# Tokens' scale inside the Gelu, small sums of the second mixer on GpSimd, a new order of the mixer's period and tail, explicit last features, and a later check of the first recurrence

## The chip, the cores and the metric

The kernel runs on one core of a Trainium2 chip. The metric is the time of one execution on the device in microseconds (us). Three runs of the kernel before took 1125.45, 1125.59 and 1127.28 us; the median is 1125.59. One more run was taken with the hardware profiler; it took 1123.8 us with a profiled span of 1122.0 us, and all stretches and durations below are of that run.

The engines are named as in the profile: PE does matrix products (PEld is its loading of weights), DVE is the vector engine, ACT the scalar engine, which applies functions such as Gelu or Sigmoid, POOL is GpSimd, and SP issues the transfers. PE writes to PSUM, and DVE and ACT take its results from there.

## The reference

The input x has 4 batches of 32 tokens, each an image of 128 x 128, all in fp32. Two layers follow each other:

```python
x = x + codano(_ln_c(x), ...)          # layer 0: attention on Fourier modes, then a mixer
t = t + ffn(_ln_t(t), W, V, ...)       # layer 0: x W, batch norm, a recurrence with a sigmoid
x = x + conv(_ln_c(x), ...)            # layer 1: upsample, leaky relu, downsample
t = t + ffn(_ln_t(t), W, V, ...)       # layer 1: the same with other weights
```

The part that the change touches most is the mixer inside `codano`:

```python
m = instance_norm(attn, norm2_g, norm2_b)
m = fno_layer(m, mixer_w1, mixer_skip_w1, mixer_skip_b1, (H, W), norm=(mixer_norm_g1, mixer_norm_b1), act=_gelu)
m = fno_layer(m, mixer_w2, mixer_skip_w2, mixer_skip_b2, (H, W), norm=(mixer_norm_g2, mixer_norm_b2))
out = instance_norm(m, mixer_out_g, mixer_out_b) + attn
```

An `fno_layer` is a convolution on 32 x 17 Fourier modes, normalised per image, plus a pointwise skip. In `ffn`, the features `x W` of all tokens are normalised by a mean and variance over everything, so the recurrence `y = sigmoid(wx + y V^T)` can't start before the last feature's statistics are in.

## The kernel before

The activations stay on the chip in `XA`, [128 rows, 4 batches, 32 tokens, 128 columns]. The features of the recurrences and its states lie in `WX`, a view of `WXY`. Stages follow each other: attention (to about 236 us), a short stretch that works out the scalars of the mixer (`f1`, `r1`, `e1`, `k1` and others), the mixer with the first features beside it (250 to 557 us), the first recurrence (to 621 us), the convolutions with the second features beside them (to about 1039 us), and the second recurrence with the output.

**The mixer** goes over 8 chunks of 4 tokens (`TM`), each of 16 images. For chunk c, `first_mixer` adds, per image, the tokens times a scale per image (`f1B`, a column for each image) to the inverse transform in PSUM (L1133, DVE, one operation per image), and applies Gelu (L1134, ACT, one operation for the four images of a batch). `transform` takes Z to its modes `Fz` (L1160, L332 on PE, copies on ACT at L1162 and L1166). `squares` (ACT, L1141) and `half_squares` (DVE, L1147) sum the squares of Z, each for half of the images. `second_mixer` is a generator of seven steps: from `Fz` and the squares it works out some numbers per image (`v2`, `x2`, `mz`, `d`, `al`, `ga`, `de`), with two inverse roots on POOL (L226, `pow`) and complex products on POOL (L1203 to L1205, L1220 to L1222), and then `G[c]`, the modes of the chunk's result (L1232, L1236 and L1237). `first_halves(of_G(c), 0)` takes G back on PE (L345), `inverse_rows` gives images in PSUM (L360), `tokens_added` adds the attention (L1246), and `residual` writes the result into XA (L1253 and L1255, two DVE operations per image). The residuals of chunk c are done during chunk c + 1 (its number is `S`).

**The first features** run behind: `chunk_stats` and `chunk_norm` give mean and inverse root of each row of a finished chunk, `rows` normalises (L290 on ACT, and L288 on DVE for some of the last tokens), `turn` transposes on PE (L296), `turned` copies (L304), `multiply` is the product (L310), and `multiplied` takes its statistics (L313, DVE) and copies it to `WX` (L317, ACT). Token u = 4(c - 2) is handled in chunk c, so two more rounds, c = 8 and c = 9, finish chunk 7's residuals and the last features.

**What sets the order.** Inside `with in_order()` PE, DVE, ACT and POOL each execute the instructions in the order in which the Python loop emits them; the loop's text is the plan. Elsewhere a scheduler orders instructions by priority. Tiles with the same tag share a fixed number of buffers: `ps4` has four PSUM buffers `big`, `psf` has one each of `t` and `w`, and `ps4s` one each of `inv10` and `inv11`.

**The recurrence** (`Recurrence.scan`) splits the 128 steps into four pieces that start from a guess and warm up over 12 steps (`WARM`); a check at its end compares where the pieces meet (L1692 to L1697 on DVE) and sets a flag that a fallback would read. The object `f1` for the second recurrence is built ahead of the first one's scan and transposes its weights then (L274, L275, copy at L277).

**The convolutions** go in units of half a token; with `at` other work is put beside a unit. The second features use the same functions `turn`, `turned` and `multiply` with one PSUM buffer `w` in the pool `ps_w` for all products.

Of the kernel before, what the change touches and what calls it, by code (L numbers as in the profile page):

```python
# [142 lines left out]
def _network(  # L143
# [249 lines left out]
    f1B, r1B = (mw.tile([P, P], F32, name=k) for k in ("f1B", "r1B"))  # L393
    q1L = mw.tile([P, NT], F32, name="q1L")
    sg, nsg = (mw.tile([P, 1], F32, name=k) for k in ("sg", "nsg"))
# [595 lines left out]
    with (  # L991
# [17 lines left out]
        def besides(n):  # L1009
# [3 lines left out]
        var, v0, r1, s, a, f1, e1, k1, q1, sv, s0 = (  # L1013
            one(k) for k in ("var", "v0", "r1", "s", "a", "f1", "e1", "k1", "q1", "sv", "s0"))
# [50 lines left out]
        tt(f1, a, scalar("mixer_skip_w1"), ALU.mult)  # L1065
# [4 lines left out]
        tt(e1, e1, a, ALU.mult)  # L1070
# [4 lines left out]
        stt(HT[:, :, :, :KW], Ym, f1, GT, ALU.mult, ALU.add)  # L1075
        nc.vector.tensor_copy(HT[:, 0, 16, 0:1], k1)
# [3 lines left out]
        for v, dst in ((f1, f1B), (r1, r1B)):  # L1080
            d = np_.tile([P, P], F32, tag="dg", name="dg")
            ts(d, ident, v, None, ALU.mult)
            p = ps3.tile([P, P], F32, tag="dg", name="ps_dg")
            mm(p, ones_sq, d, start=True, stop=True)
            nc.scalar.copy(dst, p)
# [10 lines left out]
    with (  # L1096
# [10 lines left out]
        bsum, w2d, w2s = (m1.tile([P, 1], F32, name=k) for k in ("bsum", "w2d", "w2s"))  # L1107
# [3 lines left out]
        tt(w2s, w2, w2, ALU.mult)  # L1111
        chunks = NT // TM
# [11 lines left out]
        def first_mixer(c, b, p2):  # L1124
# [5 lines left out]
            z = Z[c][:, b]  # L1130
            for i in range(TM):
                j = b * NT + c * TM + i
                stt(z[:, i], XA[:, b, c * TM + i, :], f1B[:, j : j + 1], p2[:, i], ALU.mult, ALU.add)  # L1133
            nc.scalar.activation(z, z, AF.Gelu)  # L1134


        def squares(c, images):
            for k in images:
                b, i = divmod(k, TM)
                junk = m2.tile([P, P], F32, tag="junk", name="junk")  # L1140
# [28 lines left out]
        def second_mixer(c):  # L1169
# [16 lines left out]
            for b in range(NB):  # L1186
# [7 lines left out]
            s2, s3, vm, d, al, ga, de = (  # L1194
                m1.tile([P, TM], F32, tag=k, name=k) for k in ("s2", "s3", "vm", "d", "al", "ga", "de"))
            rsqrt(s2, v2, 1e-5, TM)

            pool = nc.gpsimd.tensor_tensor
# [8 lines left out]
            ts(d, mz, nsg, None, ALU.add)  # L1207
            tt(d, d, d, ALU.mult)
            tt(vm, e2[:, :, 0], e2[:, :, 1], ALU.add)
            stt(d, vm, 1.0 / P**2, d, ALU.mult, ALU.subtract)  # L1210
            ts(d, d, w2s, None, ALU.mult)
            ts(x2, x2, w2d, None, ALU.mult)
# [9 lines left out]
            pool(G[c][:, :, 2], g1, g2, ALU.add)  # L1222
            yield True
            ts(s3, s3, scalar("mixer_out_g"), None, ALU.mult)
            ts(ga, s3, w2, None, ALU.mult)
# [3 lines left out]
            tt(al, s3, s2, ALU.mult)  # L1229
            tt(al, al, q1L[:, tr], ALU.mult)  # L1230
            ts(G[c][:, :, 0], G[c][:, :, 2], -1.0, None, ALU.mult)
            tt(G[c], G[c], al.unsqueeze(2).unsqueeze(3).broadcast_to([P, TM, 3, KH]), ALU.mult)  # L1232
            tt(de, ga, mz, ALU.mult)
            ts(de, de, -1.0, bsum, ALU.mult, ALU.add)
            tt(de, de, q1L[:, tr], ALU.mult)
            stt(G[c], Y3[:, :, :, tr].rearrange("p r k t -> p t r k"), scalar("attn_norm_g"), G[c], ALU.mult, ALU.add)  # L1236
            stt(G[c][:, :, 1, 16], de, dcm, G[c][:, :, 1, 16], ALU.mult, ALU.add)  # L1237
            ps = psf.tile([P, 512], F32, tag="t", name="ps_gb")[:, : NB * TM]
            mm(ps, ones_sq, ex.rearrange("p b t -> p (b t)"), start=True, stop=True)
            yield True  # L1240
            gB[c] = m2.tile([P, NB * TM], F32, tag="gB", name="gB")
# [6 lines left out]
        def residual(c, b, p2):  # L1248

            for i in range(TM):  # L1250
# [28 lines left out]

        def first_halves(g, t0):  # L1280
            return inverse_columns(lambda q, i, k: g(q, t0 + i, slice(k, k + 2)), ps4s, m2)
# [15 lines left out]
        def rows(t):  # L1297
            if t in range(NT) and inputs is not None:
                xn[t] = inputs.normalised(t, *norm.pop(t), vector=(t >= NT - 8 and t % 4 > 0 or t >= NT - 4))
# [22 lines left out]
        with in_order():  # L1322
# [3 lines left out]
            for c in range(chunks + 2):  # L1326
                I, S, u = c < chunks, c - 1 if 0 < c <= chunks else None, 4 * (c - 2)
                if c == chunks:
                    inputs is None or inputs.use(m2, ps4, ps4, ("big", "big"))
                multiply(u - 2)  # L1330
                turn(u - 1)
                if I:
                    first_mixer(c, 0, early_.pop((c, 0)))
                    squares(c, range(0, 2))
                    first_mixer(c, 1, early_.pop((c, 1)))
                if c in affines:
                    next(affines[c])
                if I:
                    first_mixer(c, 2, early_.pop((c, 2)))
                turned(u - 1)  # L1340
                multiplied(u - 2)
                if I:
                    first_mixer(c, 3, early_.pop((c, 3)))
                if S is not None:
                    p2 = inverse_rows(QG[S], 0, ps4)
                if I:
                    first = transform(c)
                    next(first)
                if S is not None:
                    tokens_added(S, 0, p2[0])  # L1350
                multiply(u - 1)
                if I:
                    next(first)
                    squares(c, range(2, 6))
                    half_squares(c)
                    next(first)
                    next(first)
                    next(first)
                    second = second_mixer(c)
                    next(second)  # L1360
                if S is not None:
                    residual(S, 0, p2[0])
                if I:
                    squares(c, range(6, 8))
# [632 lines left out]
```

## Time and profile before

| Stretch (us) | What | PE | DVE | ACT | POOL | Granted TensorE clock |
|---|---|---|---|---|---|---|
| 252.70 to 277.00 | chunk 0 | 18.62 | 16.16 | 9.36 | 4.68 | 0.67 |
| 305.00 to 342.00 | chunk 2 | 30.91 | 27.74 | 17.11 | 7.95 | 0.72 |
| 411.50 to 445.60 | a steady chunk | 28.41 | 29.33 | 20.23 | 7.58 | 0.85 |
| 506.20 to 532.20 | last residuals | 16.10 | 20.32 | 9.98 | 2.91 | 0.96 |
| 620.00 to 640.00 | the convolutions start | 13.78 | 17.48 | 6.77 | 3.33 | 0.91 |

The numbers under the engines are busy microseconds in the stretch. G of chunks 0 to 7 is ready at about 272.7, 299.7, 335.6, 369.2, 403.7, 437.9, 472.1 and 506.2 us, so a steady chunk takes about 34.15 us. A chain of waits is read by asking for each operation what it waited for last. A row of the groups by form names line, engine, operation, what it writes and reads, the shape, the count, and after the bar the total busy time in us and the mean in ns, then idle time ahead of it. A row of the timeline has start and length in us.

### The profile page before, as it was taken

The numbers are of one execution on the slowest core, as the hardware profiler recorded it, in microseconds if no ns is written. First come the engines' busy times: TensorE is split into PE (matmuls) and PEld (weight loads), VectorE is DVE, ScalarE is ACT, GpSimd is POOL, SyncE is SP. The second block draws the span as 40 slices with busy tenths as digits, with TensorE's granted clock in tenths as the row PEclk, the third lists the DMA queues.
The fourth block names the chain that finished last, engine by engine and source line by source line (L and its number), as shares of the span: only waits on it lengthen the run. The fifth ranks groups of instructions, "written<-read, shape, count | busy, mean of one in ns | idle before, by whom it ended". The sixth has DMA issues, their size and how long they took to land.

```text
span 1122.0 us, 18048 instructions
## 1 busy us (share of the span) xinstructions
PE 960.9 (86%) x6398; PEld 691.9 (62%) x6398; DVE 812.7 (72%) x2744; ACT 630.9 (56%) x1496; POOL 124.4 (11%) x130
## 2 busy tenths in 40 slices
PE   3999799757687777876599799999999999998896
PEld 3565566645454544542288577777777777775785
DVE  6985777756878898887488855666656666554897
ACT  3756466634347555563488444655556564655764
POOL 1000000101212122121100112020111102010000
PEclk9999799967869888889799999999999999999898
DMA  9640000010101011100000000001000000004444
GB/s 238 143 79 25 1 1 1 1 38 1 38 20 39 20 39 38 51 26 20 0 1 1 1 19 29 20 20 30 19 20 20 27 21 20 20 28 156 168 161 140
DMA packets 68964, 48.82 MB, mean 44 GB/s; under 512 B 4417, under 2 KB 63809, under 8 KB 68801
## 3 DMA queue, kind: packets, MB, share of 16 engines
q1 hardware_dynamic: 68529, 47.31, 14.8%
q8 instruction: 53, 0.87, 0.3%
q0 software_dynamic: 288, 0.01, 0.2%
q10 hardware_dynamic: 48, 0.26, 0.1%
q14 instruction: 46, 0.38, 0.1%
HBM read 30.68 MB, written 16.88 MB: 42 GB/s over the span
## 4 chain that ended last, share of the span: by engine, by line
PE 53%; DVE 22%; ACT 7%; issue 4%; POOL 4%; POOLq 0%; ACTq 0%; DVEq 0%
PE ps_scan L1657 9%; PE ps_up L1788 7%; PE ps_dn L1800 6%; PE ps_wx L310 4%; PE ps_dn L1809 3%; PE ps_up L1777 3%; PE pm L918 3%; PE ps_st L1160 3%; DVE XA L1255 3%; PE ps_y L976 2%; POOL c_r L226 2%; PE ps_inv L345 2%; DVE XA L1253 2%; DVE f_st L251 2%; DVE bn L313 2%
## 5 line engine op out<-in xcount | busy, mean ns | idle before, releaser
L1791 DVE SCALAR_TENSOR_TENSOR U<-ps_up,above 128x512 f32<-128x512 f32 x128 | 86.6, 690 | 89.9 <-ACT above L1790 89.9
L1788 PE MATMUL ps_up<-q,WXY 128*128 128x512 f32 x256 | 122.2, 599 | 6.9 <-ACT q L1780 6.5
L1800 PEld LDWEIGHTS ps_dn<-WXY,U 128*128 128x128 f32 x1024 | 124.4, 192 | 3.3
L1800 PE MATMUL ps_dn<-WXY,U 128*128 128x128 f32 x1024 | 124.6, 275 | 0.0
L1658 DVE SCALAR_TENSOR_TENSOR ps_scan<-WXY,bs,ps_scan 128x128 f32<-128x128 f32 x352 | 104.4, 353 | 10.4 <-PE ps_scan L1657 8.2
L310 PE MATMUL ps_wx<-xt,wvt 128*128 128x512 f32 x128 | 75.8, 677 | 32.1 <-ACT xt L304 27.8
L290 ACT ACTIVATE xn<-XA,f_o,f_r 128x128 f32<-128x128 f32 x178 | 75.6, 489 | 21.8 <-DVE f_o L259 21.8
L226 POOL TENSOR_TENSOR f_r<-rs_e,neg_half 128x16 f32<-128x16 f32 (+2 forms) x18 | 47.3, 2626 | 365.3 <-DVE rs_e L225 365.3
L1790 ACT ACTIVATE above<-ps_up 128x512 f32<-128x512 f32 x128 | 74.3, 597 | 23.6 <-PE ps_up L1788 23.6
L317 ACT COPY WXY<-ps_wx 128x512 f32<-128x512 f32 x64 | 37.3, 583 | 74.0 <-DVE bn L313 73.7
L1802 ACT COPY q<-ps_dn 128x512 f32<-128x512 f32 x64 | 37.5, 586 | 71.8 <-PE ps_dn L1800 71.8
L1777 PEld LDWEIGHTS ps_up<-WXY,XN 128*128 128x128 f32 x256 | 49.1, 192 | 33.6 <-issue 15.1
L1788 PEld LDWEIGHTS ps_up<-q,WXY 128*128 128x128 f32 x256 | 43.6, 190 | 40.1 <-issue 24.5
L1777 PE MATMUL ps_up<-WXY,XN 128*128 128x256 f32 x256 | 66.6, 383 | 0.0
L1809 PE MATMUL ps_dn<-q,WXY 128*128 128x256 f32 x256 | 66.0, 380 | 0.0
L313 DVE BATCH_NORM_STATS2 bn<-ps_wx 128x6 f32<-128x512 f32 x64 | 44.4, 694 | 26.7 <-PE ps_wx L310 26.6
L251 DVE BATCH_NORM_STATS2 f_st<-XA 128x6 f32<-128x128 f32 x256 | 57.8, 281 | 1.6
L1809 PEld LDWEIGHTS ps_dn<-q,WXY 128*128 128x128 f32 x256 | 46.1, 190 | 16.4 <-issue 12.0
L713 PE MATMUL ps_st<-cst,XA 128*128 128x130 f32 x256 | 43.3, 308 | 14.2 <-ACT XA L696 11.0
L304 ACT COPY xt<-ps_xt 128x512 f32<-128x512 f32 x64 | 37.6, 589 | 29.5 <-PE ps_xt L296 27.1
L310 PEld LDWEIGHTS ps_wx<-xt,wvt 128*128 128x128 f32 x128 | 22.8, 200 | 48.0 <-ACT xt L304 35.8
L713 PEld LDWEIGHTS ps_st<-cst,XA 128*128 128x128 f32 x256 | 35.0, 204 | 27.3 <-ACT XA L696 12.2
(410 smaller groups left out, 2076.2 us busy)
## 6 DMA issues: line engine op xcount, KB each, us to landing
XA<-in_x_dram SPq DMA_DIRECT2D x16, 512.0 KB, 7.3
xin<-in_x_dram SPq DMA_DIRECT2D x32, 256.0 KB, 3.2
turned<-XA SPq DMA_DIRECT2D x32, 256.0 KB, 2.3
XA<-turned SPq DMA_DIRECT2D x8, 1024.0 KB, 15.0
out_dram<-res SPq DMA_DIRECT2D x64, 128.0 KB, 2.1
WXY<-dd SPq DMA_DIRECT2D x4, 544.0 KB, 10.9
WXY<-md SPq DMA_DIRECT2D x4, 144.0 KB, 6.0
WXY<-m1d SPq DMA_DIRECT2D x1, 544.0 KB, 11.0
```

The costliest lines, as they stand in the source:

```text
L251: nc.vector.bn_stats(st[:, j * NB + b, :], XA[:, b, t, :])
L290: nc.scalar.activation(xn[:, b, :], XA[:, b, t, :], AF.Identity, bias=n(b), scale=r(b))
L310: mm(self.held[t], self.t[:, 0, :], xt, start=True, stop=True)
L713: mm(p[:, i, :], XA[:, b, t0 + j + i, :], cst[:, C_E : C_E + 130], start=True, stop=True)
L1657: mm(p4, self.t[:, 1, :], prev, start=True, stop=True)
L1658: stt(p4, WX[:, :, h, :], s[:, 0:1], p4, ALU.mult, ALU.add)
L1777: mm(p[:, b, :], XN[u // 2][:, (u % 2) * H2 + b, :], UR.rearrange("p r q -> p (r q)"), start=True, stop=True)
L1788: mm(p, UC[:, s, :], q, start=True, stop=True)
L1790: nc.scalar.activation(above, p, AF.Relu, scale=1.0 - SLOPE)
L1791: stt(U[:, s], p, SLOPE, above, ALU.mult, ALU.add)
L1800: mm(p[:, r, b, :], U[:, s, b, r * P : (r + 1) * P], DC[:, s, :], start=(s == 0), stop=(s == 1))
L1809: mm(p, DR[:, r, :], q[:, r], start=(r == 0), stop=(r == 1))
```

## The change

1. The scale per image moves from the sum to the Gelu: `first_mixer` adds `mixer_skip_w1` times the tokens to PSUM in one DVE operation per batch, and sixteen ACT operations apply Gelu with a scale (`aB`) and a bias (`k1`) that are pointers. Accordingly `f1` and one product of `e1` go, and H's constant mode is 0 where it was `k1`.
2. In `second_mixer` the sums for `d`, `x2`, `al` and `de` go from DVE to POOL; only two of G's three planes are scaled and added, and the third is their negative afterwards.
3. The loop runs over the 8 chunks alone, with its calls in another order. What followed as rounds 8 and 9 is written out as a tail. There the last chunk's features go in halves by batch pairs (`last_norm`, `last_rows`), each product covers two tokens of two batches, products use further PSUM buffers, and a Sigmoid of one column is run on ACT ahead of the last transposes. All rows of the features before that are normalised on ACT.
4. The last four products of the second features use one PSUM buffer each (`up1`, `up20`, `up21`, `up1`).
5. `check` becomes a function of its own; for the first recurrence it is emitted beside unit 5 of the convolutions. `f1` is built after the first scan is emitted.

```diff
-            for i in range(TM):
-                j = b * NT + c * TM + i
-                stt(z[:, i], XA[:, b, c * TM + i, :], f1B[:, j : j + 1], p2[:, i], ALU.mult, ALU.add)
-            nc.scalar.activation(z, z, AF.Gelu)
+            stt(z, XA[:, b, c * TM : c * TM + TM, :], scalar("mixer_skip_w1"), p2, ALU.mult, ALU.add)
+            for i in range(TM):
+                j = b * NT + c * TM + i
+                nc.scalar.activation(z[:, i], z[:, i], AF.Gelu, bias=k1, scale=aB[:, j : j + 1])
...
-            ts(d, mz, nsg, None, ALU.add)
-            tt(d, d, d, ALU.mult)
-            tt(vm, e2[:, :, 0], e2[:, :, 1], ALU.add)
-            stt(d, vm, 1.0 / P**2, d, ALU.mult, ALU.subtract)
-            ts(d, d, w2s, None, ALU.mult)
-            ts(x2, x2, w2d, None, ALU.mult)
+            pools(d, mz, nsg, None, ALU.add)
+            pool(d, d, d, ALU.mult)
+            pools(d, d, w2s, None, ALU.mult)
+            pool(ex2, e2[:, :, 0], e2[:, :, 1], ALU.add)
+            pools(ex2, ex2, w2v, None, ALU.mult)
+            pool(d, ex2, d, ALU.subtract)
+            pools(x2, x2, w2d, None, ALU.mult)
             yield True
...
+            pool(al, s2, q1L[:, tr], ALU.mult)
+            pools(al, al, scalar("mixer_out_g"), None, ALU.mult)
+            yield True
+
+            ts(ga, s3, scalar("mixer_out_g"), w2, ALU.mult, ALU.mult)
...
-            ts(G[c][:, :, 0], G[c][:, :, 2], -1.0, None, ALU.mult)
-            tt(G[c], G[c], al.unsqueeze(2).unsqueeze(3).broadcast_to([P, TM, 3, KH]), ALU.mult)
-            tt(de, ga, mz, ALU.mult)
-            ts(de, de, -1.0, bsum, ALU.mult, ALU.add)
-            tt(de, de, q1L[:, tr], ALU.mult)
-            stt(G[c], Y3[:, :, :, tr].rearrange("p r k t -> p t r k"), scalar("attn_norm_g"), G[c], ALU.mult, ALU.add)
-            stt(G[c][:, :, 1, 16], de, dcm, G[c][:, :, 1, 16], ALU.mult, ALU.add)
+            tt(al, al, s3, ALU.mult)
+            pool(de, ga, mz, ALU.mult)
+            pools(de, de, -1.0, bsum, ALU.mult, ALU.add)
+            pool(de, de, q1L[:, tr], ALU.mult)
+            pools(de, de, dcm, None, ALU.mult)
...
+            Gc = G[c][:, :, 1:3]
+            tt(Gc, Gc, al.unsqueeze(2).unsqueeze(3).broadcast_to([P, TM, 2, KH]), ALU.mult)
+            stt(Gc, Y3[:, 1:3, :, tr].rearrange("p r k t -> p t r k"), scalar("attn_norm_g"), Gc, ALU.mult, ALU.add)
+            tt(G[c][:, :, 1, 16], G[c][:, :, 1, 16], de, ALU.add)
+            ts(G[c][:, :, 0], G[c][:, :, 2], -1.0, None, ALU.mult)
...
@@ the middle of the loop, new order @@
                 if S is not None:
                     p2 = inverse_rows(QG[S], 0, ps4)
+                    tokens_added(S, 0, p2[0])
+                next(first)
                 if S is not None:
+                    tokens_added(S, 1, p2[1])
                 multiply(u - 1)
                 if S is not None:
                     residual(S, 0, p2[0])
+                    residual(S, 1, p2[1])
+                    xin.pop((S, 0))
+                load(c, 0)
+                next(first)
+                squares(c, range(0, 3))
+                next(first)
+                half_squares(c)
+                next(first)
+                multiplied(u - 1)
+                squares(c, range(3, 5))
+                if S is not None and inputs is not None:
+                    chunk_stats(S, 0)
+                next(first)
+                next(second)
+                squares(c, range(5, 8))
...
+                next(second)
+                if S is not None:
+                    residual(S, 2, p2[0], range(2))
+                next(second)
...
+                rows(u)
+                next(second)
+                if S is not None:
+                    residual(S, 2, p2[0], range(2, 4))
+                rows(u + 1)
...
@@ the end of the tail @@
+                next(halves_[0])
+                first = last_rows(S, 0, 0), last_rows(S, 0, 2)
+                inputs.use(m2, ps4, ps4s, ("big", "inv11"))
+            multiplied(u + 2)
+            multiply(u + 3)
+            if inputs is not None:
+                nc.scalar.activation(m1.tile([P, 1], F32, name="one"), bsum, AF.Sigmoid, scale=0.0)
+                turns = [inputs.turn(xn_) for xn_ in first]
+                multiplied(u + 3)
...
@@ second features and check @@
+                if t >= NT - 4:
+                    f1.use(wk, ps_t, ps_c1, ("t", ("up1", "up20", "up21", "up1")[t - NT + 4]))
                 f1.products(t, xt.pop(t))
...
+            at(5, f0.check)
...
             f1.scan(output)
+            f1.check()
```

## The prediction

> **What bounds the kernel now.** I read the busy line of the page first: no engine is full over the whole span, so the stages must be looked at one by one.
>
> ```profile
> PE 960.9 (86%) x6398; PEld 691.9 (62%) x6398; DVE 812.7 (72%) x2744; ACT 630.9 (56%) x1496; POOL 124.4 (11%) x130
> ```
>
> Then the busy times of single stretches: one steady period of the mixer loop, then the stretch from the last residual to the first recurrence.
>
> ```profile
> 445.60:479.80 34.20, 28.42 (x252) 17.90 (x252) 29.44 (x119) 20.23 (x53) 7.73 (x11) 0.85 0.17 47
> ...
> 532.20:557.00 24.80, 14.60 (x38) 6.86 (x38) 11.16 (x36) 11.69 (x25) 3.11 (x2) 0.74 0.00 0
> ```
>
> After the length come the busy times of PE, PEld, DVE, ACT and POOL with their counts, then the granted clock. In the loop DVE works 29.4 of 34.2 us; in the tail nobody works half the time and TensorE is granted 0.74. The chain of waits within one period says what the period is made of (time, length, who):
>
> ```profile
> 438.06 3.69 PE ps_inv L345 x64
> ...
> 445.02 0.71 DVE bn L313
> ...
> 446.88 1.12 PE ps_wx L310 x2
> ...
> 448.44 1.06 PE ps_inv L360 x4
> 449.50 1.93 PE ps_st L1160 x16
> ...
> 455.61 1.09 PE ps_pf L332 x28
> 456.72 0.38 ACT Fz L1166
> 457.13 0.42 ACT sq L1174
> 457.58 0.30 DVE sq L1176
> ...
> 471.83 0.24 DVE G L1237
> 472.20 0.87 PE ps_inv L345 x9
> ```
>
> It is a ring of 34.1 us: G ready (438.0), its transform on PE, the next Z, Gelu, two forward transforms, Fz, small sums, G again (472.1). Until 457.5 it passes between PE, ACT and DVE; from there it is DVE in order. So it counts when Fz is ready and what DVE does on the path, not busy time alone. Last, the rows that price the change, from the groups by form, and the end of the second features in the timeline:
>
> ```profile
> L1133 DVE SCALAR_TENSOR_TENSOR Z<-XA,f1B,ps_inv 128x128 f32<-128x128 f32 x128 | 34.6, 341 | 9.6 <-PE ps_inv L360 9.6
> L1134 ACT ACTIVATE Z<-Z 128x512 f32<-128x512 f32 x32 | 19.8, 625 | 7.1 <-DVE Z L1133 6.4
> L290 ACT ACTIVATE xn<-XA,f_o,f_r 128x128 f32<-128x128 f32 x178 | 75.6, 489 | 21.8 <-DVE f_o L259 21.8
> ...
> 1033.21 1.90 PE L310 MATMUL ps_wx<-xt,wvt 128*128 128x512 f32 x2 [1.41 <-ACT WXY L317]
> 1035.15 0.70 DVE L313 BATCH_NORM_STATS2 bn<-ps_wx 128x6 f32<-128x512 f32 x1 [2.61 <-PE ps_wx L310]
> 1035.89 0.58 ACT L317 COPY WXY<-ps_wx 128x512 f32<-128x512 f32 x1 [2.73 <-DVE bn L313]
> 1036.52 0.50 PEld L310 LDWEIGHTS ps_wx<-xt,wvt 128*128 128x128 f32 x2 [2.98 <-ACT WXY L317]
> ```
>
> The last four lines are one turn of a ring through a single PSUM buffer: product, statistics, copy, next product, 3.3 us each.
>
> **What the Trainium skill says.** "ScalarE: Activation LUTs", section "What ACT_TABLE_LOAD costs": an ACTIVATE costs 186 ns plus 0.833 ns per element, 93 ns more per pointer operand, and neighbours overlap by 93. That is 479 ns for 128 columns with scale and bias as pointers; the trace agrees (L290, 489 ns; four in 1.64 us, 0.385 apart). The same section gives about 1283 ns for a table load; this trace has 1.28 us at 559.78. "GPSIMD Engine Reference", section 3.1, puts a two-input GpSimd operation at about 2.6 cycles per element of 1.2 GHz, 277 ns for 128 columns; the 128x128 products here (456 ns) then leave an estimated 0.18 us fixed. "TensorE: Matmul & The Clock Gate", Part 1, says that idle stretches halve the clock; here the same pair of products takes 1.12 us after short gaps and 2.08 at 534 us after 7.2 us of idling.
>
> **The change part by part.** All sums are against the profiled span, 1122.0 us; that run took 1123.8, the others 1125.45 to 1127.28 with median 1125.59. I put G at zero in the period that begins at 438.0.
>
> *Gelu with scale and bias.* DVE: 16 operations at 0.27 apart (4.3 us) become four of 128x512, as L1791 (690 ns, 0.62 apart): 2.5. DVE wins 1.8 us a chunk. ACT: four of 0.63 become sixteen 0.385 apart, 6.2 us. ACT has room in sum (20.2 of 34.2), but Gelu lies on the ring. Z starts at 7.6 as before; ACT is free at 8.7; three images, a copy of xt and one of a product, the last image: 8.7+4.65+1.0+1.6 = 15.9, before 13.1.
>
> *Order of the period.* In the new order of instructions both residuals of the first pair, the half squares and the statistics of a product come ahead of the ring's small sums on DVE. The first residual waits for PE (product 8.8, turn, inverse rows to 11.4, tokens added 12.3), where before DVE had the half squares to do. From 12.3 DVE runs 2.6+2.6+2.3+0.6 = 8.1 to 20.5. ACT's copy of that product is queued ahead of Fz, so Fz (pf is ready at 19.6) waits for it: copy 0.5, two squares 1.0, Fz and its square 0.8: 22.9, before 19.5. The parts take 1.35: 24.3, before 20.8.
>
> *Small sums on GpSimd.* DVE loses about 1.0 us (L1207 to L1212) and 1.1 us in the part with G (128x384 to 128x256, three de operations, one al). But the sums become a wait. DVE from 24.3: two residual images 1.3, sa and rs_e 0.3, GpSimd starts at 26.1; pow 1.0, three products 1.4 (as 462.47 to 464.86), then seven operations of 128x4, the last of which gives x2. DVE has two images (1.3) and two small operations, then stands at x2. The trace has no such operation: a memset of 128x4 takes 0.10 (lower end), the 128x128 product 0.456 (upper end). I take 0.20 from the 0.18 above: 1.4, x2 at 29.9, a wait of 2.2 us. Behind DVE's wait stand the last residual, G, and with G all of PE's next inverse. Then three sums and rs_e 0.7, residual 2.6 (beside it pow 1.0, products 1.45, two al operations 0.4 on GpSimd), ga and ex 0.4, al 0.2, G 0.45+0.6+0.2+0.25: 35.4.
>
> So the steady period is 35.4 against 34.15: **+1.25**. DVE's work falls from 30.8 (dense, gaps of issue included) to 26.9, its idle rises from 3.3 to 8.5. Six periods (chunks 2 to 7): +7.5. Chunk 1 has no features: ACT's longer Gelu +1.5, residuals leave the path, +0.6. Chunk 0 has nothing to hide with: Gelu +1.7, squares and sums on the path, +2.9. Two small operations ahead of the loop go: -0.4. **Loop: +10.6.** Loads of xin, on SP's queue, move with the residuals that free their buffers; they land in 3.2 us, half a period ahead of use, so nothing. The statistics of the chunk before rows are needed run beside PE's transform of G: nothing.
>
> *The tail.* Before: G of the last chunk 506.2, last residual ends 532.2, last statistics 556.7, thus 50.5. After: PE brings the first residual at 12.2; DVE is then dense, four residuals 10.4, three statistics 1.8, first half's row statistics 2.8: 27.3. Second half: 2.8, GpSimd pow of 8 columns 1.64 and 0.35 around it: 32.0. ACT is then the limit: four rows to 33.4, copy 0.5, table load and its dummy 1.55, copy 0.5, two turned copies 1.05 to 37.0, four rows to 38.6, four half copies to 40.0, two turned copies to 41.0, last product 42.6, statistics 43.4. **-7.1.** The spans of the first halves are hidden by DVE's residuals.
>
> *Start of the recurrence.* The table load (1.28) no longer stands between DVE at 559.7 and the first step, and a weight copy (L277, 0.43, 0.3 effective) leaves DVE: **-1.6**. The copy and its two transposes move into the first steps, where PE waits for ACT anyway.
>
> *Check of the first recurrence.* Of its operations the order keeps the first (differences, product) at the old place; comparison and reduction (0.42 and 0.67) leave the path between 622.6 and 625.9: **-1.0**. They land in the convolutions, where PE is busy 98% and DVE 63%: nothing.
>
> *Last four features.* With own PSUM banks the products don't wait for copies. Rows of the last image are normalised by 1027.1 as now; then xt copies 1027.7 and 1029.3 (two product copies between them), product 1030.4, statistics 1031.2, before 1039.37: **-8.1**. Output then starts at 1053.7 instead of 1061.7; the 8 MB read into XA is issued by 1039.6 and DMA is quiet from 1053, so it isn't in the way.
>
> Sum: 10.6-7.1-1.6-1.0-8.1 = **-7.2**, a span of 1114.8; from the median, **1118.4 us**.
>
> **Rivals.** (1) *Slower: the GpSimd sums decide.* Each 0.1 us more per small operation adds 0.7 at x2 and 0.2 at al, over 8 chunks 7.2 us. At 0.30 the change is even; at 0.40 it costs +7.2, 1132.8; at the upper end 0.456, 1136.8. For it: scalar pointers, and DVE and GpSimd hinder each other here (L1214 takes 0.41 beside a product, 0.21 alone). Against: the fixed part above. At the lower end 0.10 the time is 1111.2.
> (2) *The period does shrink.* If the waits I place at 12.3, 22.9 and 29.9 mostly vanish, DVE's 26.9 and the idle of before (3.3) bound it: about 31, six times -3.2, chunk 0 and 1 even: -19 and the ends -17.8: 1089. For it: that DVE is busiest. Against: the ring above.
> (3) *The ends are hidden anyway.* PE at half clock (2.1 us per product) or another buffer takes half of the 17.8: -8.9+10.6 = +1.7, 1127.3. For it: 0.74 granted there. That the change doesn't do what it says is excluded for instructions, since the built order shows each part, for time it is this case.
>
> **How the numbers follow.** What this kernel's measurement can tell from no change is 0.2%, 2.3 us. Forecast 0.54 (own range 1110 to 1125), rival 1 0.24, rival 2 0.12, rival 3 0.10. Faster: 0.47+0.12+0.02 = 0.61; same: 0.06+0.04+0.05 = 0.15; slower: 0.01+0.20+0.03 = 0.24. The range 1103 to 1135 leaves out rival 2 and the top of rival 1.
>
> **What would show it.** Right: sixteen Gelus near 0.49 us, DVE idle before x2 with GpSimd as releaser about 2 us per chunk, G to G near 35.4, the last four feature products about 1 us apart where they were 2.5 to 3.3, no table load at the first recurrence. Wrong: periods under 34, small GpSimd operations at 0.3 us or more, or features still 2.5 us apart at the end.

## The result, and the profile after

The changed kernel takes 1131.25 us (median of 8 runs, 1129.52 to 1132.40), the kernel before 1127.2, measured beside it: a ratio of 1.0034, 95% interval 1.0022 to 1.0046. It is slower by 0.3%; 1118.4 and "faster" were forecast. The two profiled executions differ by 5.7 us (1122.0 and 1127.7), where the forecast's sum was -7.2, and the loss is not where that sum would put it. Marks for the table are the first transform of H1 by 56 products, the first product on G of the last chunk, the last statistics (`mv`) of the first and of the second features, and the first `c_o` of the convolutions:

| stretch | before | after | difference | forecast |
|---|---|---|---|---|
| start to H1 | 246.60 | 250.21 | +3.6 | -0.4 |
| H1 to the last G (loop) | 259.75 | 275.78 | +16.0 | +11.0 |
| last G to first `mv` (tail) | 50.39 | 44.14 | -6.3 | -7.1 |
| `mv` to first `c_o` (recurrence, check) | 70.26 | 67.28 | -3.0 | -2.6 |
| `c_o` to second `mv` (convolutions, last features) | 412.37 | 406.66 | -5.7 | -8.1 |
| second `mv` to the end | 82.63 | 83.63 | +1.0 | 0 |
| sum | 1122.0 | 1127.7 | +5.7 | -7.2 |

The busy line of the page shows that what was meant to move did move:

```profile
PE 960.8 (85%) x6398; PEld 689.9 (61%) x6398; DVE 788.4 (70%) x2561; ACT 668.4 (59%) x1605; POOL 155.1 (14%) x235
```

DVE has 24.3 us less to do, ACT 37.5 and GpSimd 30.7 more. The stretch table of one steady period and of the tail after the last residual (17.40 us, where it was 24.80) says what came of it (from, to, length, then busy PE, PEld, DVE, ACT, POOL, the granted clock):

```profile
452.62:488.99 36.37, 28.63 (x252) 17.96 (x252) 26.51 (x96) 24.03 (x65) 11.46 (x23) 0.86 0.16 45
552.70:570.10 17.40, 10.19 (x31) 5.21 (x29) 9.78 (x33) 11.05 (x27) 1.99 (x2) 0.80 0.00 0
```

The period grew from 34.2 to 36.4 us while DVE's work in it fell from 29.4 to 26.5. So DVE waits. The chain of waits of this period has a stretch that was not there before:

```profile
478.47 1.01 POOL s L226
479.48 0.51 POOL g L1202
479.99 0.42 POOL g L1203
480.41 0.07 issue
480.48 0.46 POOL G L1204
480.93 0.30 POOL d L1206
...
482.75 0.28 POOL sa L1212
483.03 0.02 issue
483.06 0.17 DVE vm L1216
```

GpSimd does a pow, three products of 128x128 and then seven sums of 128x4 in its own order; the last of them (x2, a part of the tile `sa`) releases DVE. The groups by form say how long each takes and how long DVE stood:

```profile
L1133 ACT ACTIVATE Z<-Z,k,aB 128x128 f32<-128x128 f32 x128 | 50.7, 486 | 1.2 <-DVE Z L1130 1.2
L1206 POOL TENSOR_SCALAR d<-sa,nsg 128x4 f32<-128x4 f32 x8 | 2.5, 310 | 0.0
L1207 POOL TENSOR_TENSOR d<-d 128x4 f32<-128x4 f32 x8 | 1.6, 202 | 0.7
L1216 DVE TENSOR_TENSOR vm<-vm,sa 128x4 f32<-128x4 f32 x8 | 1.3, 164 | 21.1 <-POOL sa L1212 21.1
L1233 POOL TENSOR_SCALAR de<-de,bsum 128x4 f32<-128x4 f32 x8 | 4.0, 495 | 0.9
L1242 DVE TENSOR_TENSOR G<-G,de 128x4 f32<-128x4 f32 x8 | 1.3, 167 | 3.6 <-POOL de L1235 3.1 <-POOL SQ L1128 0.5
```

A two-input sum takes 0.20 us, one with a pointer 0.30, and one beside DVE's update of G 0.49. DVE stands 21.1 us in all at x2, 2.6 per chunk, and 3.6 more ahead of the sum of G with `de`.

The 3.6 us ahead of the loop come from a stage of which no line changes. ACT's timeline of the attention stage, first after, then before:

```profile
102.05 1.28 ACT L1019 ACT_TABLE_LOAD   x1
103.34 0.20 ACT L1019 ACTIVATE sg<-k 128x1 f32<-128x1 f32 x1
114.54 1.28 ACT L232 ACT_TABLE_LOAD   x1
115.83 0.20 ACT L232 ACTIVATE rq_q<-rq_e 128x4 f32<-128x4 f32 x1
```

```profile
113.97 0.20 ACT L232 ACTIVATE rq_q<-rq_e 128x4 f32<-128x4 f32 x1 [0.34 <-DVE rq_e L231]
...
208.16 1.28 ACT L1019 ACT_TABLE_LOAD   x1
209.45 0.20 ACT L1019 ACTIVATE sg<-k 128x1 f32<-128x1 f32 x1
```

The Gelu of one element that makes sg moved from 208 to 102 us, between two square roots, and the second of them must load its table again. That stage is ordered by the scheduler. The four transposes of Pm that end the gram stage start at 136.32 after and at 131.26 before, 5.1 us later. The load itself is 1.28 us of that; the larger part is an order on PE. Its timeline, first after, then before:

```profile
115.34 3.95 PE L799 MATMUL pg<-WXY 128*64 128x64 f32 x64
119.21 0.73 PE L749 MATMUL ps_fr<-FF,WXY 32*128 32x272 f32 x2
```

```profile
114.67 0.75 PE L749 MATMUL ps_fr<-FF,WXY 32*128 32x272 f32 x2 [0.15 <-ACT WXY L750]
115.36 5.43 PE L799 MATMUL pg<-WXY 128*64 128x64 f32 x64
```

The last two products of `ps_fr` now stand behind the 64 of `pg`. Their copy on ACT (L750) and DVE's L756 behind it start at 119.98 and 120.40, where before they started at 115.46 and 115.89: 4.5 of the 5.1 us.

At the end, PE's timeline shows the products of the last four features:

```profile
1038.13 2.88 PE L310 MATMUL ps_wx<-xt,wvt 128*128 128x512 f32 x6
1042.18 1.12 PE L310 MATMUL ps_wx<-xt,wvt 128*128 128x512 f32 x2 [0.73 <-ACT xt L304]
```

Three products in 2.88 us and the fourth after it, where before they were 2.5 to 3.3 us apart.

### The profile page after: what moved, and what is told of

Same layout as the page of the kernel before. It is cut to its first block, busy times and chain, and to the rows that moved or that the text cites. A ratio compares the mean times of both kernels' runs of the same rounds, so it can differ in the third digit from the quotient of the medians.

```text
span 1127.7 us, 18109 instructions
## 1 busy us (share of the span) xinstructions
PE 960.8 (85%) x6398; PEld 689.9 (61%) x6398; DVE 788.4 (70%) x2561; ACT 668.4 (59%) x1605; POOL 155.1 (14%) x235
## 3 DMA queue, kind: packets, MB, share of 16 engines
q1 hardware_dynamic: 68529, 47.31, 14.6%
## 4 chain that ended last, share of the span: by engine, by line
PE 46%; DVE 17%; issue 15%; POOL 11%; ACT 9%; DMA 1%; SPq 0%; POOLq 0%; ACTq 0%; DVEq 0%
PE ps_scan L1747 9%; PE ps_up L1889 7%; PE ps_dn L1901 6%; POOL f_r L226 3%; PE ps_up L1878 3%; PE ps_dn L1910 3%; PE ps_st L713 2%; PE ps_wx L310 2%; PE ps_y L976 2%; PE pm L918 2%; POOL c_r L226 2%; DVE U L1892 2%; DVE f_st L251 2%; ACT above L1891 2%; POOL s L226 1%
## 5 line engine op out<-in xcount | busy, mean ns | idle before, releaser
L310 PE MATMUL ps_wx<-xt,wvt 128*128 128x512 f32 x128 | 73.5, 665 | 25.3 <-ACT xt L304 25.3
L290 ACT ACTIVATE xn<-XA,f_o,f_r 128x128 f32<-128x128 f32 x176 | 73.9, 491 | 21.1 <-DVE f_o L259 21.0
L1903 ACT COPY q<-ps_dn 128x512 f32<-128x512 f32 x64 | 37.5, 586 | 71.8 <-PE ps_dn L1901 71.8
L1878 PEld LDWEIGHTS ps_up<-WXY,XN 128*128 128x128 f32 x256 | 49.6, 194 | 34.8 <-issue 15.9
L251 DVE BATCH_NORM_STATS2 f_st<-XA 128x6 f32<-128x128 f32 x240 | 54.5, 282 | 1.6
L1256 DVE SCALAR_TENSOR_TENSOR XA<-ps_inv,r1B,xin 128x128 f32<-128x128 f32 x128 | 44.2, 345 | 12.8 <-PE ps_inv L1249 12.8
L713 PEld LDWEIGHTS ps_st<-cst,XA 128*128 128x128 f32 x256 | 35.6, 208 | 27.4 <-ACT XA L696 12.3
L1133 ACT ACTIVATE Z<-Z,k,aB 128x128 f32<-128x128 f32 x128 | 50.7, 486 | 1.2 <-DVE Z L1130 1.2
```

What stands on the lines that cost most here:

```text
L251: nc.vector.bn_stats(st[:, j * NB + b, :], XA[:, b, t, :])
L310: mm(self.held[t], self.t[:, 0, :], xt, start=True, stop=True)
L713: mm(p[:, i, :], XA[:, b, t0 + j + i, :], cst[:, C_E : C_E + 130], start=True, stop=True)
L1878: mm(p[:, b, :], XN[u // 2][:, (u % 2) * H2 + b, :], UR.rearrange("p r q -> p (r q)"), start=True, stop=True)
```

## The experiments

Three theories were open: the table order ahead of the loop against chance between executions; GpSimd's sums against the Gelu and the new order in the loop; and whether the ends bring what the forecast says. Each ratio is against runs of the kernel before on the same chip, measured beside the run (their median was 1126.8 to 1130.1 us); the other times come from one profiled execution of a spread, so a ratio and a difference of spans need not agree. "Loop" is from H1 to the last G.

| run | ratio (95%) | span | H1 at | loop |
|---|---|---|---|---|
| before | 1 | 1122.0 | 246.60 | 259.75 |
| after | 1.0034 (1.0022 to 1.0046) | 1127.7 | 250.21 | 275.78 |
| e1 table | 0.9957 (0.9936 to 0.9978) | 1121.5 | 248.25 | 274.94 |
| e2 sums on DVE | 0.9861 (0.9825 to 0.9898) | 1109.0 | 248.45 | 262.95 |
| e3 products first | 0.9873 (0.9840 to 0.9905) | 1114.0 | 248.33 | 262.43 |
| e4 ends only | 0.9801 (0.9768 to 0.9835) | 1108.5 | 247.04 | 260.75 |
| e5 Gelu only | 0.9976 (0.9964 to 0.9989) | 1122.3 | 247.94 | 276.68 |
| e6 order, old Gelu | 0.9861 (0.9831 to 0.9891) | 1107.0 | 246.91 | 262.19 |
| e7 GpSimd sums only | 0.9894 (0.9869 to 0.9920) | 1111.2 | 247.05 | 265.85 |
| e8 old order, shorter G | 0.9810 (0.9784 to 0.9836) | 1102.2 | 248.66 | 256.62 |
| e9 k1 alone | 1.0051 (1.0025 to 1.0077) | 1131.7 | 251.88 | 260.29 |
| e10 statistics later | 0.9968 (0.9952 to 0.9984) | 1121.8 | 249.43 | 272.32 |
| e11 third chunk | 0.9927 (0.9903 to 0.9951) | 1117.1 | 249.35 | 270.79 |
| e12 first chunks | 0.9770 (0.9739 to 0.9801) | 1102.4 | 248.71 | 252.11 |

**e1: the table.** From after:

```diff
-        tt(k1, scalar("norm2_b"), scalar("mixer_skip_w1"), ALU.mult)
+        k0 = one("k1")
+        tt(k0, scalar("norm2_b"), scalar("mixer_skip_w1"), ALU.mult)
...
-        nc.scalar.activation(sg, k1, AF.Gelu)
+        nc.scalar.activation(sg, k0, AF.Gelu)
...
+        nc.vector.tensor_copy(k1, k0)
```

> The changed kernel with one edit: the constant whose Gelu gives sg goes back into a tile of the pool of the last attention stage (as in the kernel before) and is copied into the long-lived k1 later, on DVE. Theory (the new place of k1 let the scheduler hoist its Gelu from 208 us to 102 us, between two square roots, so that a square root's table is loaded once more at 114.5 and the gram stage ends 4 us later): no Gelu table at 102, no second square root table, the first step of the mixer (first inverse transform of H1) back near 246.9, span 3.5 to 4 us below the changed kernel's 1127.7, so about +1.5 to +2 us against the kernel before; the loop from there to the last G stays at 275 us. Rival (the 3.6 us ahead of the loop are chance between executions): H1 stays at 250, span within 1 us of 1127.7.

The two extra loads are gone, and the transposes of Pm start at 131.18 (136.32 after, 131.26 before):

```profile
131.18 1.09 PE L880 MATMUL ps_pt<-ident,Pm 128*128 128x128 f32 x4 [5.59 <-DVE Pm L876]
```

H1 falls by only 2.0 us, since the stretch from those transposes to the last mean (`ps_e`) took 104.6 us in this execution, 103.0 before and 101.4 after. The difference of 1.6 from before is not of the edit: the same code took 103.0 in e4, e6 and e7, and 104.6 to 104.9 in e8 and e10 to e12. The low value after may be: that stretch is without sg's Gelu and its load there. This was not tested apart. The loop is as long as after. The span is 6.2 us below after's, more than the 3.5 to 4 expected: the tail gives 1.3 of it, the part from the first `mv` on 2.1, the loop 0.8. Against the kernel before, the ratio says 0.4% faster, where 1.5 to 2 us slower were expected; the spans are within 0.5 us.

**e9: the same edit alone, in the kernel before.**

```diff
-    sg, nsg = (mw.tile([P, 1], F32, name=k) for k in ("sg", "nsg"))
+    k1, sg, nsg = (mw.tile([P, 1], F32, name=k) for k in ("k1", "sg", "nsg"))
...
-        var, v0, r1, s, a, f1, e1, k1, q1, sv, s0 = (
+        var, v0, r1, s, a, f1, e1, q1, sv, s0 = (
```

> The kernel before with one edit: the constant k1 lives in the long-lived pool instead of that of the last attention stage. No operation is added or removed by hand; the built order has the Gelu of one element at the place between two square roots again, with two more table loads. Theory (the table order costs, not chance): the gram stage's transposes of Pm start 4 to 5 us later (131.3 before), the span is 3 to 5 us longer, ratio 1.003 to 1.005. Rival (what e1 gave back was chance, or hidden): within 1 us.

The transposes of Pm start at 136.43 and the kernel is slower by 0.5%. Where a 128x1 tile is allocated costs 5 us of that stage. The products of `pg` and `ps_fr` stand in the order of the kernel after here, and in e1 in that of the kernel before. The span is 9.7 us longer, twice what was expected: 5.3 at H1, and 3.9 in the tail, which has before's instructions at a granted clock of 0.72 instead of 0.85. Chance is ruled out for the gram stage: they start at 136.3 and 136.4 in the two kernels whose Gelu for sg reads a tile of the long-lived pool, at 130.9 to 132.1 in the other twelve.

**e2: the small sums back on DVE** (from e1, thirteen operations, GpSimd keeps pow and products):

```diff
-            pools(d, mz, nsg, None, ALU.add)
...
-            pools(x2, x2, w2d, None, ALU.mult)
+            ts(d, mz, nsg, None, ALU.add)
...
+            ts(x2, x2, w2d, None, ALU.mult)
```

> As e1_table, and the thirteen small sums of the second mixer that the change gives to GpSimd run on DVE again (six, two and four operations, with the two pow operations and the six 128x128 products staying on GpSimd); order, Gelu and ends as in the changed kernel. Theory (GpSimd's sums decide the longer loop): the waits of 2.6 us at x2, 1.1 at al and 0.45 at de go, 1.0 to 1.8 us of DVE work comes back of which a part lies in the first pow: steady period 36.4 to about 34.3, eight chunks -14 to -16 us against e1_table, so about 12 us below the kernel before. Rival (the new order of the period and the longer Gelu decide, GpSimd's sums are covered): period 36 to 36.4, within 3 us of e1_table. At least the third of the period before the sums (Fz at 22.0 us after G) is the same in both.

The loop is 12.0 us shorter than in e1 (274.94 to 262.95), most periods 34.9. In the new order GpSimd's sums are three quarters of the loop's +16.0. The last copy of Fz starts 21.9 us after G, as after (22.0): the gain is all behind it. The period stays 0.6 above the 34.3 expected, and one took 37.2: in it a pair of products took 2.07 us at a granted clock of 0.50 instead of 1.13.

**e3: the same sums on GpSimd, but its products ahead of the first pow, and x2 the first of the sums** (from e1).

```diff
             nc.scalar.square(sq, Fz[c])
             yield True
+            pool(g1, wr, Fz[c][:, 0], ALU.mult)
...
+            pool(G[c][:, :, 2], g1, g2, ALU.add)
...
+            pools(x2, x2, w2d, None, ALU.mult)
             pools(d, mz, nsg, None, ALU.add)
```

> As e1_table, GpSimd keeps every sum, but its six 128x128 products with Fz are issued ahead of the first pow, right after Fz's square, when GpSimd stands idle, and x2 is the first of the seven small sums. Theory (it is GpSimd's queue, 1.4 us of products ahead of 2.1 us of small sums, not the single small operation): DVE's wait at x2 shrinks from 2.6 to below 0.5 and one of about 1 us comes at d; the second pow ends 1.6 us earlier, al waits less by about 1: period 36.4 to about 34, -16 to -20 us against e1_table. If small operations are as slow as they look because DVE's traffic holds them, they stay at 0.2 to 0.5 us each. Rival (order and Gelu decide): period stays at 36.

GpSimd's timeline in one period:

```profile
425.88 0.45 POOL L1182 TENSOR_TENSOR g<-m,Fz 128x128 f32<-128x128 f32 x1 [16.49 <-ACT Fz L1167]
...
428.50 0.49 POOL L1187 TENSOR_TENSOR G<-g,g 128x128 f32<-128x128 f32 x1
429.69 1.02 POOL L226 TENSOR_TENSOR s<-rs_e,neg_half 128x4 f32<-128x4 f32 x1 [0.70 <-DVE rs_e L225]
430.70 0.39 POOL L1210 TENSOR_SCALAR sa<-sa,w2d 128x4 f32<-128x4 f32 x1
...
432.68 0.20 POOL L1216 TENSOR_TENSOR d<-ex,d 128x4 f32<-128x4 f32 x1
433.36 1.04 POOL L226 TENSOR_TENSOR s<-rs_e,neg_half 128x4 f32<-128x4 f32 x1 [0.48 <-DVE rs_e L225]
```

All six products are done before DVE asks for the pow. The groups by form have 0.8 us of waiting at x2 over eight chunks (21.1 after) and 9.6 at d:

```profile
L1222 DVE TENSOR_TENSOR vm<-vm,d 128x4 f32<-128x4 f32 x8 | 1.3, 163 | 9.6 <-POOL d L1216 9.6
L1220 DVE TENSOR_TENSOR vm<-vm,sa 128x4 f32<-128x4 f32 x8 | 1.3, 163 | 0.8
```

The loop is 12.5 us shorter than in e1, with every sum still on GpSimd at the same 0.2 to 0.5 us each. It was the place in the queue that cost, not the engine. The loop is as long as e2's; what each of the two moves brought was not tested apart.

**e4: the ends only** (before's loop and mixer; tail, checks, second recurrence and last features of the change):

```diff
-            for c in range(chunks + 2):
+            for c in range(chunks):
...
+            S, u = chunks - 1, NT - 8
...
+            at(5, f0.check)
```

> The kernel before with its own loop, its Gelu and its small sums on DVE, and only the ends of the change: the new tail after the last chunk with the table load in it, the check of both recurrences later, second recurrence set up after the first, own PSUM banks for the last four features. Theory: periods stay at 34.15 and the last G near 506; from there to the last statistics 44.7 instead of 50.5, first step 1.5 sooner, check 0.8, last features 7.5 of which about 1 to 2 is lost again within the convolutions: span 14 to 15 us below the kernel before, ratio 0.986 to 0.989. Rival 3 of the prediction (the ends are hidden anyway): half of it or less, ratio above 0.993.

The span falls by 13.5 us, a little under the 14 to 15 expected, since chunk 0 took 3.0 us longer than before at a lower granted clock (0.50 against 0.69 from 250 to 280). That is 1.2%; the ratio, 0.980, is below the 0.986 to 0.989 expected. Rival 3 is out.

**e5: e4 and the Gelu with scale and bias** (k1 as in e1; the scratch tile `junk` has one buffer, as in the changed kernel, here and in e7 and e8).

```diff
-            for i in range(TM):
-                stt(z[:, i], XA[:, b, c * TM + i, :], f1B[:, j : j + 1], p2[:, i], ALU.mult, ALU.add)
-            nc.scalar.activation(z, z, AF.Gelu)
+            stt(z, XA[:, b, c * TM : c * TM + TM, :], scalar("mixer_skip_w1"), p2, ALU.mult, ALU.add)
+            for i in range(TM):
+                nc.scalar.activation(z[:, i], z[:, i], AF.Gelu, bias=k1, scale=aB[:, j : j + 1])
```

> e4_ends_only with one more part of the change: the Gelu per image with scale and bias, DVE's Z in four operations of 128x512; order of the period and small sums as before. Theory (the Gelu lies on the ring on ACT): Fz, 18.4 us after G in e4, comes about 2.5 us later, DVE wins 1.8 us a chunk, and the period goes from e4's 33.7 to 34 to 35, six periods and chunk 0 together +5 us against e4. Rival (DVE sets the period): DVE's 1.8 us come off, period near 32, -8 us against e4.

The loop grows by 15.9 us over e4, far more than either theory said; periods are 35.8 to 36.9. DVE's timeline shows why: in the old order the half squares come right behind Z, and now they wait for ACT twice per period. These waits are 14.0 us in the last five periods, none in e4, and the five grew by 13.1.

```profile
429.26 1.45 DVE L1148 BATCH_NORM_STATS2 zst<-Z 128x6 f32<-128x128 f32 x4 [1.84 <-ACT Z L1135]
431.75 1.45 DVE L1148 BATCH_NORM_STATS2 zst<-Z 128x6 f32<-128x128 f32 x4 [1.05 <-ACT Z L1135]
```

**e6: e2 with the old Gelu** (e5's diff the other way, in the new order).

> e2_sums_on_dve (new order of the period, sums on DVE, ends of the change) with the old Gelu: sixteen DVE operations with the token's scale, a Gelu of 128x512. Theory (after GpSimd's sums, the rest of the longer period is the Gelu): Fz, 22.1 us after G in e2, comes about 2 us sooner and the period goes from 34.9 to about 33.5, -8 us against e2. Rival (it is the order: residuals, half squares and a product's statistics ahead of the ring's sums on DVE, the product's copy ahead of Fz on ACT): Fz stays at or above 22 us, since DVE has 1.8 us more ahead of it, and the period is 35 to 36.5, +2 to +10 us against e2.

The loop is 262.19 against e2's 262.95; Fz stays at 21.9 and the period at 34.9, with two of 37.2 and 37.6 in place of e2's one: the order sets it, as the rival says, though its 2 to 10 us more did not come either. In the new order the residuals of the first pair stand between Z and the half squares, so ACT's longer Gelu is covered and DVE's 1.8 us bring nothing. The two edits belong together: the Gelu alone costs 15.9, in the new order 0.8. That 0.8 is a net figure: with the old Gelu chunk 0 is 3.0 shorter, at a granted clock of 0.63 instead of 0.56, and the last chunk, one of the long periods, 2.3 longer.

**e7: e4 and GpSimd's sums, in the old order** (the mixer of the changed kernel; it also has its shorter G).

> e4_ends_only with one more part of the change: the small sums on GpSimd behind its products, and G in the changed form; order of the period and Gelu as before. Theory (a queue of 1.0 us pow, 1.4 us products and 2.1 us of small sums stands ahead of DVE's x2, whatever the order): DVE waits 1.5 to 3 us at x2 and about 1 at al, less what the residual and statistics placed there cover; period 33.7 to 35 to 36, +8 to +16 us against e4. Rival (the wait exists only with the new order, since in the old one a pair's statistics of 1.6 us stand ahead of x2 and cover it): within 3 us of e4.

The loop grows by 5.1 us over e4, period 34.5 to 35.2, so the size lies between the two theories. The wait does not:

```profile
L1218 DVE TENSOR_TENSOR vm<-vm,sa 128x4 f32<-128x4 f32 x8 | 1.3, 162 | 19.8 <-POOL sa L1214 19.8
```

DVE stands at x2 nearly as long as after (21.1), so the queue is not of the new order, and the rival is out. The theory left out what DVE saves: in one period the wait is 2.4 us, but DVE's own sums are 1.0 and its part with G 0.8 shorter. In chunks 3 to 7 the sums cost 5.3 us here and 6.1 in the new order (e1 against e2); the two orders differ in chunks 0 to 2, by -0.2 and 5.9. There e4's chunk 0 had a granted clock of 0.50 and e7's 0.74, so that part is not settled.

**e8: a candidate**, old order, sums on DVE, shorter G:

```diff
-                    if inputs is not None:
-                        chunk_stats(S, 0)
...
                 multiplied(u)
+                if S is not None and inputs is not None:
+                    chunk_stats(S, 0)
```

> A candidate for the best: e4_ends_only with the changed form of G (two of three parts computed, the third by negation, al prepared ahead of the second pow) but all small sums on DVE, and the statistics of the first pair of images (1.55 us) moved from between the small sums to behind the statistics of the product that follows G, where DVE idles 2.5 to 3 us. Theory (from Fz to G the ring is DVE in order): 1.5 + 0.6 us leave it, period 33.7 to about 31.7, six or seven periods -12 to -15 us against e4, near 1095 in the profile. Rival (the ring of products on PE and their copies is as long, so a new wait comes): period not below 33.

The span is 1102.2, the loop 4.1 us shorter than e4's; periods are 33.2 to 35.2, not 31.7. The rival was nearer: the next product's statistics now wait behind 3.1 us of rows' statistics.

**e10 and e11** tried to mend that:

```diff
-                if c in affines:
-                    next(affines[c])
...
+                if c in affines:
+                    next(affines[c])
                 rows(u)
...
+                multiplied(u + 1)
                 if S is not None and inputs is not None:
                     chunk_stats(S, 2)
...
-                multiplied(u + 1)
```

That is e10; e11 adds the new body for chunk 2.

> e8_old_order_shorter_G with the statistics of the second pair and the sums of the rows' norm moved behind the second product's statistics, and the norm's last operation moved from between the images' Z to just ahead of its first use. Theory (in e8 that product's statistics wait 1 us for DVE, and its copy, the next xt and the next product on PE with it): period from 33.3, sometimes 34.9, to about 32.5 with fewer stretches of half clock, -4 to -6 us against e8. Rival (DVE is dense, 29.5 us of 33.2 busy, so what is moved out of one gap fills another): within 1.5 us of e8.

> e10_old_order_stats_later with chunk 2 alone, the first with features, in the order of the changed kernel. Theory (from G of chunk 1 to G of chunk 2 the old order takes 34.7 us in e8, the new one 29.2 in e6): -4 to -5 us against e10. Rival (the work only moves over the border of the chunk): chunk 3 gives it back, within 1.5 us of e10.

Neither worked as meant. In e10 the product's statistics come first, but 2.8 us of other statistics stand directly ahead of Z, which starts 9.9 us after G instead of 7.9; periods grow to 38. In e11 chunk 2 alone in the new order took 36.9 us, as in e10 (36.8): its profit in e6 is not its own. e11's span is 4.7 us below e10's, as forecast, but by luck: the loop gave 1.5, through chunk 3, and the tail 2.0 with the same instructions at a granted clock of 0.95 instead of 0.80.

**e12: e8 with chunks 0 to 2 in the new order**, the others in the old one (`if c <= 2:` and the new body ahead of the old).

> e8_old_order_shorter_G with chunks 0 to 2 (the third is the first with features) in the order of the changed kernel, chunks 3 to 7 in the old one. Theory (the new order is the better one only where no feature product waits for DVE: from the first transform of H1 to G of chunk 2 it takes 82.7 us in e6 and 86.6 in e8, while the old order's later periods of 33.2 to 34.9 are the shorter ones): -3 to -5 us against e8's span of 1102.2. Rival (the work moves over the border): chunk 3 takes it back, within 1.5 us of e8.

The loop is 4.5 us shorter than e8's, as the theory has it, but the span is the same: the tail took 47.2 us instead of 43.7, with the same instructions at a granted clock of 0.69 instead of 0.95. With 0.977 (0.974 to 0.980) it is the best ratio, not told apart from e4 and e8 by the intervals. All three beat both kernels, by 1.9 to 2.3% against before.

## Why the prediction was wrong

The forecast is off by 12.9 us in the span: 4.0 ahead of the loop, 5.0 in it, 0.9 in the tail, 2.4 in the convolutions with the last features, 1.0 at the end, and -0.4 at the recurrence. The single steps that failed are a term put at nothing ahead of the loop, and GpSimd's queue, left out in chunk 1 and priced too low in the others.

*Ahead of the loop: the step that failed outright.* The prediction wrote "Two small operations ahead of the loop go: -0.4" and named no cost for k1's new tile. It costs 5.1 us at the end of the gram stage (e1, e9); at H1 it is 2.0 to 5.3 (e1, e9), and 3.6 between before and after. Only edits to operations were priced; the place of a tile is an edit too where a scheduler orders the code, and the built order of ACT, two table loads longer, told it. The prediction's own line on tables counted the load at 559.78 only.

*The loop: rival 1, by another route.* GpSimd's sums cost 12.0 us (e1 against e2). Within the steady period the sum held up to the pow, and not by luck: the first residual was placed at 12.3 after G and starts at 12.4, the end of Fz's square at 22.9 and is at 22.8, the pow at 26.1 and is at 25.85. From there to x2 it took 4.6 us and not 3.8, because seven sums last 2.1 us with their gaps and not 1.4 (mean of one 0.26, not 0.20); from x2 to G 5.9 and not 5.5, because the four operations on `de`, which had no price in the sum, end 0.45 behind DVE. So the period is 36.4 and not 35.4, and the wait at x2 2.6 and not 2.2. Rival 1 made it a question of the small operation's price, with even at 0.30. At the measured 0.26 its own rule, 9 operations of 8 chunks, adds 4.3 us to the forecast, which would still leave the change 2.9 faster. What e3 shows is that the queue decides: with the products out of the way and x2 first, the same sums cost no more than on DVE.

*The six steady chunks* were forecast at +7.5 together and measured +7.2 (213.69 against 206.54), but not as six equal steps: chunk 2 fell from 36.0 to 31.1, and the five others grew by 2.4 each. The nearness of the sum is luck, two errors that cancel: +1.25 was forecast for each, and no term made chunk 2 shorter. It is shorter in every kernel with the whole loop in the new order, and in e12; why stayed open. So the loop's miss of 5.0 is in chunks 0 and 1, forecast at +2.9 and +0.6 and measured +5.4 and +3.5. For GpSimd's queue the forecast had no term in chunk 1, and in chunk 0 at most 1.2 us for squares and sums together; GpSimd's sums cost 3.3 us in chunk 0 and 1.5 in chunk 1 (e1 against e2). For the rest of chunk 0 the granted clock is a candidate, as e4 lost 3.0 there with before's own loop; it was not tested apart.

*The Gelu and the order* (rival 2 hoped they would shrink the period). Fz comes 3.3 us later after G than before, as forecast (3.4). With the sums on DVE, e2's loop is 3.2 us longer than before's, and this too is a sum of opposites: +2.1 and +1.4 in chunks 0 and 1, -6.9 in chunk 2, +6.6 in the last five. e6's is 2.4 us longer.

*The ends were right.* The tail gave 6.3 of 7.1, recurrence and check 3.0 of 2.6. The last features gave 5.7 of 8.1 in this execution; but from `c_o` to the second `mv` the kernels e1, e2, e5 to e8 and e12, with the same end, took 404.4 to 404.5, which is -7.9. Executions e3 and after had 406.7 there, e4 405.7, from the same instructions; what sets it stayed open. The +1.0 at the end is within what kernels with the same end took there, 81.3 to 84.2. So rival 3 is refuted, and e4 alone is worth 2.0% by ratio, 1.2% by span. One sentence of the prediction was wrong on its own evidence: in the tail of before "nobody works half the time", while PE was busy 14.6 of 24.8 us.

The Trainium skill had two of the points. "ScalarE: Activation LUTs", section "Rules for kernel authors", says to do all functions of one table set before switching; here the switch was the scheduler's, and 1.28 us of load came with 5.1 us of stage. "SBUF — State Buffer", section "Who interferes with whom", says that a DVE instruction with two SBUF inputs contends with a GpSimd instruction that reads SBUF. The trace agrees for `de`: 0.49 us (L1233) beside DVE's scaling of G, which reads two tiles of SBUF, 0.30 for the same kind of operation elsewhere.

## What to carry to other kernels

Work moved to an idle engine joins a queue: price what stands ahead of it there, not only its own time, in every stage where it runs, and issue first what another engine waits for. The same sums made the loop 12 us longer behind three products, and no longer than on DVE with the products out of the way and the awaited sum first. Read the built order of every engine over the whole program, table loads included, even where the diff touches no line: here a tile with a longer life moved an instruction by 100 us. A sum that comes out right over a group of chunks is not yet a right sum: look at each.

## What the runs showed that was not expected

The granted TensorE clock did not follow the length of the gap ahead of a product. In the tail of e8 pairs of products took 1.13 and 1.12 us after idling 2.04 and 2.39, and in e12, with the same instructions, 2.07 and 2.08 after 0.68 and 1.04. PE's timeline of e8 first, then of e12:

```profile
510.52 1.13 PE L310 MATMUL ps_wx<-xt,wvt 128*128 128x512 f32 x2 [2.04 <-ACT xt L304]
514.48 1.12 PE L310 MATMUL ps_wx<-xt,wvt 128*128 128x512 f32 x2 [2.39 <-ACT xt L304]
```

```profile
506.23 2.07 PE L310 MATMUL ps_wx<-xt,wvt 128*128 128x512 f32 x2 [0.68 <-ACT xt L304]
510.20 2.08 PE L310 MATMUL ps_wx<-xt,wvt 128*128 128x512 f32 x2 [1.04 <-ACT xt L304]
```

From 500 to 506.5 us the granted clock is 0.50 in both; from 507 to 513 it is 1.00 in e8 and 0.50 in e12. PE had idled before these rows, 5.82 us to 502.88 in e8 and 4.19 us to 498.74 in e12. So the prediction's point from "TensorE: Matmul & The Clock Gate", Part 1, that idle stretches halve the clock, is not contradicted; but the gap just ahead of a product does not tell the clock of that product. Why it stayed at half longer in e12 was not tested. A stage of many short gaps differed by 3.5 us between two kernels that run the same code in it, so single profiles are to be compared by stretches, not by spans.
